# First layer of a two-layer kernel: scan output summed by transposes, layer norm with positions on partitions, gate projections of 32 rows, and one ordered plan

## The chip, the cores and the metric

The kernel runs on one core of one Trainium2 chip. The metric is the device time in microseconds (us) of one execution, lower is better; several executions are timed and their median is compared. The core has a matrix engine (PE, with its weight loads shown apart as PEld), a vector engine (DVE), an activation engine (ACT), a general engine (POOL) and a queue engine that issues transfers (SP). Each works through its own list of instructions in order, and they wait for one another by semaphores. PE writes to PSUM, which has eight banks of 2 KB per partition here; POOL reads and writes SBUF alone.

## The reference

Two layers one after the other, on x of 8 x 192 x 64 x 64, all in fp32. The change is in the first; the second (layer norm over 192 channels and two state-space scans, forward and flipped) stays as it is. The first layer, per image:

```python
x = conv1x1(x, W_in)                          # 192 -> 384 channels
x = depthwise_conv3x3(x, W_dw) + b_dw
x_proxy = conv1x1(x, W_xd)                    # 16 channels
ws, Ls, Us, Ds = (conv1x1(x_proxy, w) for w in (W_w, W_l, W_u, W_d))
xs = [x, x.T, flip(x), flip(x.T)]             # 4 directions
Gl, Gm, Gr = ws[:nd], ws[nd:2*nd], ws[2*nd:]
s = abs(Gl) + abs(Gm) + abs(Gr) + 1e-7        # each gate is divided by s
# scan over 8 columns (j) of each of the 8 chunks of a row:
#   h = l * x + gl * h_up + gm * h + gr * h_down
out = gate_scan(xs, Ls, Gl, Gm, Gr, 8)
out = out * Us + xs * Ds
y = einsum('bdchw,d->bchw', out, w_m)         # sum over the 4 directions
y = layernorm2d(y, ln_w, ln_b)                # over the 384 channels
y = grn(y, gamma, beta)                       # global norm over positions per channel
return conv1x1(y, W_out)                      # 384 -> 192
```

## The kernel before, in words

The 384 channels lie on partitions as 3 tiles of 128 (c = 0, 1, 2). An image goes through three stages.

**Units** (class `Image`). There are 24 units, one for each c and each band r of 8 rows (512 positions). `begin` is two accumulating matmuls into a PSUM bank (tags gl, gm, q, yp in turn), three ACT passes (the middle tap with the bias, and the taps at the two sides) and two POOL additions; the other six taps of the 3 x 3 convolution are six DVE operations in `unit`. `proxy` projects a finished band to 16 channels, held four times, at partitions 0, 32, 64 and 96, as tile xp.

**Scan** (class `Step`). For each c, each j (0 to 7) and each direction d (0 to 3) there is one step on tiles of 128 x 512: 96 steps per image, 12 of them with j = 0, where the state begins and most parts do nothing. The parts of a step with j > 0 are:

- `gates`: four matmuls of 16 rows (`gate`), pl for the input's factor and g[0..2] for the three neighbours, each with its weights at another 32-row group. `up`: two more, pd and pu.
- `decay` (ACT copies pl to lam), `entry` (POOL: lam times x), `magnitude` (ACT: absolute values; that of g[2] in place), `norm` (DVE: two additions), `log`, `exp` (ACT), `newton` (DVE: two operations) for 1/s.
- `neighbour` 0, 1, 2 (DVE: gate times shifted state), `pair` (POOL: q0 + q1), `total` (PE: q2 + q0 by the identity), `mix` (DVE: times 1/s), `state` (POOL).
- `direct` (ACT copies pd), `bypass` (POOL: times x; for d = 3 it also adds the dx of d = 2, `JOINED`), `output` (DVE: pu times the state, giving hu).
- `add`: PE adds hu and dx into the bank yp by the identity, over the four directions of one j; the dx of d = 2 is left out since it is in that of d = 3. `store`: ACT copies yp to y after d = 3.

PSUM tags: gl, gm, q, yp have one bank each; gr and c have two. pl, pd and pu all take the tag "c". The state of a step is read by the step four later (same direction, next j).

The order on each engine is the program order (`manual_schedule`); across engines Tile puts in the waits, also for a PSUM slot that is still to be read. In `scan` the order is written out by hand: in one turn of the loop stand `s3`, `s2`, `s1`, `s0` and `ahead`, five steps one apart, and each part stands once.

**Norm and projection** (class `Norm`, `project_out`) of an image run while the units of the next one do: per j, three matmuls with a matrix of 1/384 give the mean on all partitions, DVE subtracts, ACT squares, three more matmuls give the variance, ACT and DVE make the inverse root, POOL scales, and ACT squares with a sum over positions for the global norm. `PARTS` and the loop at the end say how many units and projections stand between one another. After the last image the norm and the projection stand alone. The result goes to `mid` in DRAM, which the second layer reads.

Of the kernel before, what the change touches and what calls it, by code (L numbers as in the profile page):

```python
# [8 lines left out]
F32 = mybir.dt.float32  # L9
# [24 lines left out]
JOINED = 2  # L34
# [3 lines left out]
PARTS = [0] * 8 + [1, 1, 1, 2, 1, 1, 1, 1, 1, 1, 1, 1, 1, 1, 1, 1]  # L38
# [4 lines left out]
ROWS = {GL: (0, 0), GM: (1, 0), GR: (2, 0), GLAM: (3, 0), GU: (0, 1), GD: (1, 1)}  # L43

# [78 lines left out]
def kernel(ctx: ExitStack, tc: tile.TileContext, x, w_in, dw, vecs, w_xd, w_gate, w_m, w_out, mid):  # L123
# [9 lines left out]
    big = ctx.enter_context(tc.tile_pool(name="l0_big", bufs=6))  # L133
# [32 lines left out]
    w_gate_sb = const.tile([P, 2, ND, CI], F32, name="w_gate_sb")  # L166
    for kind, (group, at) in ROWS.items():
        nc.sync.dma_start(w_gate_sb[32 * group : 32 * group + RANK, at], w_gate[:, kind])
# [10 lines left out]


# [9 lines left out]
    class Image:  # L190
# [6 lines left out]
        def __init__(self, b):  # L197
            self.b = b
            self.x = x[b].rearrange("(k p) h w -> p k (h w)", p=KM)
            self.xc, self.xins, self.banks = [], {}, {}  # L200
            self.xp = p1.tile([P, CHUNK, CHUNK, HW], F32, tag="xp", name=f"xp_{b}")
            self.u = 0
            for u in range(4):
                self.load(u)
            for u in range(2):
                self.begin(u)
# [7 lines left out]
        def begin(self, u):  # L214
            c, r = divmod(u, CHUNK)
            if r == 0:
                self.xc.append(big.tile([P, HW, HW], F32, tag="big", name=f"xc_{self.b}_{c}"))
# [5 lines left out]
            self.load(u + 4)  # L223
# [26 lines left out]
        def proxy(self, r):  # L250
            pp = bank("c", f"pp_{self.b}_{r}")
            for c in range(NC):
                nc.tensor.matmul(
                    pp,
                    w_xd_sb[:, c, :],
                    self.xc[c][:, 8 * r : 8 * r + 8, :].rearrange("p h w -> p (h w)"),
                    start=(c == 0),
                    stop=(c == NC - 1),
                )
            nc.scalar.copy(  # L260
                self.xp[:, :, :, 8 * r : 8 * r + 8].rearrange("p j n h -> p h n j"),
                pp.rearrange("p (h n j) -> p h n j", n=CHUNK, j=CHUNK),
            )

        def unit(self):

            u, self.u = self.u, self.u + 1
            if u + 2 < UNITS:
                self.begin(u + 2)
            c = u // CHUNK  # L270
            for t in (0, 1, 2, 6, 7, 8):
                acc, part = self.shifted(u, t)
                nc.vector.scalar_tensor_tensor(
                    acc, part(self.banks[u]), dw_sb[:, c, t : t + 1], acc, ALU.mult, ALU.add
                )
            if u >= UNITS - CHUNK + 2:
                self.proxy(u % CHUNK - 2)
# [17 lines left out]
    class Step:  # L295
# [4 lines left out]
        def __init__(self, tag, xc, xp, wg, d, j):  # L300
            self.tag, self.xc, self.xp, self.wg, self.d, self.j = tag, xc, xp, wg, d, j
# [7 lines left out]
        def gate(self, kind, tag):  # L309
# [3 lines left out]
            r = slice(32 * group, 32 * group + RANK)  # L313
            nc.tensor.matmul(dst, self.wg[r, at, self.d, :], flat(self.xp[r, self.j]), start=True, stop=True)  # L314
# [37 lines left out]
        def norm(self):  # L352
            if self.j:
                for i in range(2):
                    nc.vector.tensor_add(self.g[2], self.g[2], flat(self.ab[i]))  # L355
# [11 lines left out]
        def newton(self):  # L367

            if self.j:
                s, rc = self.g[2], flat(self.rc)  # L370
                nc.vector.scalar_tensor_tensor(s, s, 1e-7, rc, ALU.add, ALU.mult)
                nc.vector.scalar_tensor_tensor(rc, s, 2.0, rc, ALU.subtract, ALU.mult)
# [16 lines left out]
        def bypass(self):  # L389
            nc.gpsimd.tensor_mul(self.dx, self.dx, direction(self.xc, self.d, self.j))  # L390
            if self.d == JOINED + 1:
                nc.gpsimd.tensor_add(self.dx, self.dx, self.before.dx)
# [5 lines left out]
        def add(self, i):  # L398


            if self.d == 0 and i == 0:
                self.yp = bank("yp", f"yp_{self.tag}")
            elif i == 0:
                self.yp = self.before.yp
            if i == 0 or self.d != JOINED:
                nc.tensor.matmul(
                    self.yp,
                    ident,
                    flat((self.hu, self.dx)[i]),
                    start=(self.d == 0 and i == 0),  # L410
                    stop=(self.d == ND - 1 and i == 1),
# [6 lines left out]
    class Nothing:  # L418


        def __getattr__(self, part):
            return lambda *args: None

    def scan(b, xc, xp):


        ys, steps = [], [Nothing()] * 4
        for c in range(NC):
            wg = w_gate_sb[:, :, :, c * P : (c + 1) * P]
            ys.append(big.tile([P, CHUNK, CHUNK * HW], F32, tag="big", name=f"y_{b}_{c}"))  # L430
            for j in range(CHUNK):
                steps += [Step(f"{b}_{c}_{j}_{d}", xc[c], xp, wg, d, j) for d in range(ND)]
                for step in steps[-ND:]:
                    step.y = ys[c][:, j, :]
        for before, step in zip(steps[4:], steps[5:]):
            step.before = before
        steps += [Nothing()] * 4
        for s3, s2, s1, s0, ahead in zip(steps, steps[1:], steps[2:], steps[3:], steps[4:]):
            s2.state()
            s0.neighbour(2)  # L440
            s0.neighbour(0)
            s0.entry()
            s1.newton()
            s1.total()
            s0.neighbour(1)
            s0.pair()
            s0.magnitude(2)
            s2.direct()
            ahead.gates()
            s0.norm()  # L450
            s0.log()
            ahead.decay()
            s2.bypass()
            s3.add(0)
            s2.output()
            s3.add(1)
            ahead.magnitude(0)
            s1.up()
            s0.exp()
            s1.mix()  # L460
            ahead.magnitude(1)
            s3.store()
        return ys

    class Norm:


        def __init__(self, b, ys):
            self.b, self.ys = b, ys
            self.ss = p1.tile([P, NC, CHUNK], F32, tag="ss", name=f"ss_{b}")  # L470
            self.pm, self.squares, self.var, self.rstd = {}, {}, {}, {}

        def mean(self, j):
            self.pm[j] = bank("gr", f"pm_{self.b}_{j}")
            for c in range(NC):
                nc.tensor.matmul(self.pm[j], mean_w, self.ys[c][:, j, :], start=(c == 0), stop=(c == NC - 1))

        def center(self, j):
            for c in range(NC):
                y = self.ys[c][:, j, :]  # L480
                nc.vector.tensor_sub(y, y, self.pm[j])
                sq = self.squares[j, c] = p2.tile(
                    [P, T], F32, tag=("ab0", "ab1", "dx")[c], name=f"sq_{self.b}_{j}_{c}"
                )
                nc.scalar.activation(sq, y, AF.Square)

        def variance(self, j):
            self.var[j] = bank("c", f"pv_{self.b}_{j}")
            for c in range(NC):
                nc.tensor.matmul(self.var[j], mean_w, self.squares[j, c], start=(c == 0), stop=(c == NC - 1))  # L490

        def root(self, j):

            r = self.rstd[j] = p2.tile([P, T], F32, tag="rc", bufs=3, name=f"rstd_{self.b}_{j}")
            v = self.var[j]
            nc.scalar.activation(r, v, AF.Ln, bias=eps5)
            nc.scalar.activation(r, r, AF.Exp, scale=-0.5)
            nc.vector.scalar_tensor_tensor(v, v, 1e-5, r, ALU.add, ALU.mult)
            nc.vector.tensor_mul(v, v, r)
            nc.vector.scalar_tensor_tensor(r, v, 3.0, r, ALU.subtract, ALU.mult)  # L500

        def response(self, j):

            for c in range(NC):
                y = self.ys[c][:, j, :]
                sq = p2.tile([P, T], F32, tag="hu", name=f"sq2_{self.b}_{j}_{c}")
                nc.scalar.activation(
                    sq,
                    y,
# [6 lines left out]
        def scale(self, j):  # L516
            for c in range(NC):
                y = self.ys[c][:, j, :]
                nc.gpsimd.tensor_mul(y, y, self.rstd[j])

        def parts(self):

            for j in range(CHUNK + 2):
                if j < CHUNK:
                    self.mean(j)
                if 0 <= j - 1 < CHUNK:
                    self.root(j - 1)
                    self.scale(j - 1)
                if j > 1:
                    self.response(j - 2)  # L530
                if j < CHUNK:
                    self.center(j)
                yield
                if j < CHUNK:
                    self.variance(j)

    def project_out(b, ys, ss):

        gr = p1.tile([P, NC + 1], F32, tag="gr", name=f"gr_{b}")
        gx, rg = gr[:, :NC], gr[:, NC:]  # L540
        nc.vector.tensor_reduce(gx, ss, AX.X, ALU.add)
        nc.scalar.activation(gx, gx, AF.Sqrt)
        nc.scalar.preload_act_table_set(ACT_SET)
        yield
        pg = bank("c", f"pg_{b}", (P, 1))
        for c in range(NC):
# [564 lines left out]
```

## Time and profile before

| | |
|---|---|
| median of 3 runs | 16562.87 us (16551.99 to 16567.64) |
| the profiled execution | 16565.53 us, its span 16563.7 us |
| mean granted clock of PE | 0.923 of full |
| busy, whole span | PE 14978.0, DVE 14708.4, ACT 11718.0, POOL 14908.0 us |
| last transfer to `mid` issued (first layer ends) | 5978.3 us |
| stores of y of image 2, first and last | 1652.8 and 2175.8 us |
| first store of y of image 3 | 2383.5 us |

A line of a group view reads: line, engine, operation, out<-in by the program's names, shapes, count, then busy us and mean ns of one, then the idle time of the engine just before them and what ended most of it. A line of the timeline reads: start us, duration us, engine, line, operation, operands, count, and in brackets the idle time before it and what ended that. A matmul with fp32 operands is two records on PE, a transpose one. Ends of PE's records are modelled, so starts are the better measure there.

### The profile page before, as it was taken

What the parts mean: (1) busy time and instruction counts of PE and PEld (TensorE: products, weight loads), DVE (VectorE), ACT (ScalarE), POOL (GpSimd) and SP (SyncE); (2) the same over time, 40 slices, a digit from 0 to 9 for tenths busy, and PEclk for the clock granted to TensorE, in tenths of its full rate; (3) what the DMA queues carried; (4) which work ended last, traced back from release to release, by engine and by line L of the source; (5) the groups of instructions that cost most, each with busy time, mean ns of one, the idle gap of its engine ahead of it and who ended that gap; (6) DMA issues with size and microseconds to landing.
All of it is one profiled execution on the core that took longest, in us unless ns stands there. A gap on an engine that the chain in (4) does not pass through costs nothing.

```text
span 16563.7 us, 198688 instructions
## 1 busy us (share of the span) xinstructions
PE 14978.0 (90%) x66768; PEld 8677.0 (52%) x66768; DVE 14708.4 (89%) x13970; ACT 11718.0 (71%) x25475; POOL 14908.0 (90%) x9292
## 2 busy tenths in 40 slices
PE   9999999999999978888888888888888888888888
PEld 2333333333333346666666666666666666666666
DVE  8887888788888859999999999999999999999999
ACT  5666666666656657777777777777777777777777
POOL 7887979787787859999999999999999999999999
PEclk8999999999999989999999999999999999989999
DMA  1001010100000012222323232222222222222232
GB/s 30 21 11 31 1 31 1 31 11 21 27 4 27 1 61 109 108 109 111 115 110 116 108 113 109 108 109 108 109 108 109 108 109 108 109 108 112 108 115 98
DMA packets 732369, 1260.72 MB, mean 76 GB/s; under 512 B 346905, under 2 KB 415345, under 8 KB 731345
## 3 DMA queue, kind: packets, MB, share of 16 engines
q1 hardware_dynamic: 730944, 1247.72, 20.6%
q8 instruction: 526, 8.62, 0.2%
q14 instruction: 499, 4.08, 0.1%
q10 hardware_dynamic: 400, 0.29, 0.0%
HBM read 1189.11 MB, written 58.72 MB: 75 GB/s over the span
## 4 chain that ended last, share of the span: by engine, by line
POOL 23%; PE 10%; ACT 10%; DVE 9%; issue 6%; DMA 4%; SPq 0%; POOLq 0%; DVEq 0%; ACTq 0%
POOL hs L963 16%; DVE da L979 5%; POOL hs L986 5%; PE pc L785 4%; ACT da L969 3%; DMA b_sb<-bc 3%; DVE hs L979 2%; PE yp L991 2%; PE pz L795 2%; PE pj L864 2%; DVE hs L986 2%; POOL dtx L877 1%; DMA c_sb<-bc 1%; ACT xc L806 1%; ACT z L807 1%
## 5 line engine op out<-in xcount | busy, mean ns | idle before, releaser
L963 POOL TENSOR_TENSOR hs<-dtx,b_sb 128x1022 f32<-128x1022 f32 x3072 | 7183.6, 2361 | 139.1 <-DMA b_sb<-bc 118.4
L979 DVE TENSOR_TENSOR_SCAN da<-da,hs 128x1024 f32<-128x1024 f32 x2048 | 4686.7, 2288 | 408.3 <-POOL hs L963 309.4
L969 ACT ACTIVATE da<-dt,a 128x512 f32<-128x512 f32 x6144 | 4247.6, 691 | 61.8
L991 PE MATMUL yp<-ident,hs 128*128 128x128 f32 x24576 | 3377.6, 290 | 89.7 <-POOL hs L986 68.6
L991 PEld LDWEIGHTS yp<-ident,hs 128*128 128x128 f32 x24576 | 2993.9, 150 | 625.9 <-issue 359.4
L979 DVE TENSOR_TENSOR_SCAN hs<-da,hs 128x1024 f32<-128x1024 f32 x1024 | 2314.1, 2280 | 316.4 <-ACT da L969 228.1
L986 DVE TENSOR_TENSOR hs<-da,c_sb 128x1024 f32<-128x1024 f32 x2048 | 2499.9, 1221 | 62.2 <-DVE da L979 0.5
L986 POOL TENSOR_TENSOR hs<-hs,c_sb 128x1024 f32<-128x1024 f32 x1024 | 2418.5, 2362 | 3.9 <-ACT state L982 3.9
L785 PE MATMUL pc<-xT,conv 128*128 128x512 f32 x4608 | 2165.2, 603 | 69.3 <-ACT xT L758 66.7
L314 PE MATMUL g<-xp,w_gate_sb 16*128 16x512 f32 x8640 | 1817.2, 658 | 60.4 <-ACT dx L387 51.6
L340 DVE TENSOR_TENSOR q<-g,h 128x512 f32<-128x512 f32 x2016 | 1353.1, 685 | 117.8 <-PE g L314 71.2
L350 PE MATMUL q<-q,ident 128*128 128x512 f32 x2688 | 1337.7, 620 | 0.0
L785 PEld LDWEIGHTS pc<-xT,conv 128*128 128x128 f32 x4608 | 813.5, 191 | 981.4 <-issue 858.1
L360 ACT ACTIVATE rc<-g,eps 128x512 f32<-128x512 f32 x672 | 462.0, 688 | 1114.2 <-DVE g L355 1114.2
L390 POOL TENSOR_TENSOR dx<-dx,xc 128x512 f32<-128x512 f32 x768 | 1079.9, 1406 | 156.9 <-ACT dx L387 133.4
L982 ACT COPY state<-da 128x2 f32<-128x2 f32 x2048 | 322.8, 158 | 1267.2 <-DVE hs L986 1256.6
L314 PEld LDWEIGHTS g<-xp,w_gate_sb 16*128 16x128 f32 x8640 | 494.0, 188 | 1308.0 <-DVE q L340 392.2
L864 PE MATMUL pj<-ident,lg 128*128 128x128 f32 x1536 | 555.5, 362 | 561.3 <-ACT lg L858 561.3
L344 POOL TENSOR_TENSOR q<-q,q 128x512 f32<-128x512 f32 x672 | 853.6, 1270 | 199.5 <-DVE q L340 193.7
L334 POOL TENSOR_TENSOR lam<-lam,xc 128x512 f32<-128x512 f32 x672 | 942.7, 1403 | 32.9 <-ACT lam L331 32.9
L355 DVE TENSOR_TENSOR g<-g,ab 128x512 f32<-128x512 f32 x1344 | 933.5, 695 | 22.8
L795 PE MATMUL pz<-in_w,xT 128*128 128x384 f32 (+1 forms) x2048 | 855.6, 520 | 82.4 <-ACT xc L787 79.1
(148 smaller groups left out, 26031.3 us busy)
## 6 DMA issues: line engine op xcount, KB each, us to landing
b_sb<-bc SPq DMA_DIRECT2D x1024, 512.0 KB, 10.2
c_sb<-bc SPq DMA_DIRECT2D x1024, 512.0 KB, 10.1
xin<-in_x_dram SPq DMA_DIRECT2D x192, 384.0 KB, 3.6
mid<-ot SPq DMA_DIRECT2D x128, 192.0 KB, 2.1
xt<-mid SPq DMA_DIRECT2D x64, 384.0 KB, 10.0
out_dram<-y SPq DMA_DIRECT2D x64, 384.0 KB, 9.9
xt<-mid SPq DMA_DIRECT2D x64, 128.0 KB, 9.1
bc<-dbl SPq DMA_DIRECT2D x128, 64.0 KB, 1.7
```

What stands on the lines that cost most here:

```text
L314: nc.tensor.matmul(dst, self.wg[r, at, self.d, :], flat(self.xp[r, self.j]), start=True, stop=True)
L334: nc.gpsimd.tensor_mul(self.lam if self.j else self.hc, self.lam, direction(self.xc, self.d, self.j))
L340: nc.vector.tensor_mul(self.q[i], rows(self.g[i]), self.h[:, :, i : i + HW])
L350: nc.tensor.matmul(self.sum, ident, flat(term), start=(i == 0), stop=(i == 1))
L390: nc.gpsimd.tensor_mul(self.dx, self.dx, direction(self.xc, self.d, self.j))
L785: nc.tensor.matmul(self.pc[c], w[:, n, :], x[:, k, at : at + T], start=(n == 0), stop=(n == 5))
L795: nc.tensor.matmul(pi, self.tokens.xT[r, i, 3 + s * P : 3 + (s + 1) * P], self.m.in_w[r, i, :], start=(i == 0), stop=(i == 1),)
L963: nc.gpsimd.tensor_mul(self.hs[:, :, 1:], dtx, self.p.b_sb[self.g][:, :, 1:])
L969: nc.scalar.activation(self.da[:, n, :], self.p.dt[self.c], AF.Exp, scale=self.p.m.a[:, self.c, at : at + 1])
L979: nc.vector.tensor_tensor_scan(h, da, hs, 0.0, ALU.mult, ALU.add)
L986: engine.tensor_mul(self.hs, self.h, self.p.c_sb[self.g])
L991: nc.tensor.matmul(self.p.yp[self.c][:, s, :], self.hs[:, n, s * P : (s + 1) * P], ident, is_transpose=True, start=False, stop=(self.g == ...
```

## The change

- The order of the whole first layer comes from tables of slots. Every part of every unit, step and norm gets a number (its base plus the table's entry) and all are issued in the order of these numbers. Step k of an image stands at slot 28 + k, and images are 128 slots apart. `newton` and `norm` are split into their two operations.
- `add` turns hu and dx in four pieces of 128 x 128 by transposing matmuls that accumulate in yp, so y has positions on partitions and channels along the free dimension. The joined dx is gone.
- Layer norm: `bn_stats` and `bn_aggr` over 384 channels per block of 128 positions, an inverse root of small tiles per two j, scaling on POOL, and `back`, which transposes to channels on partitions (12 transposes per j) and copies and squares from PSUM on ACT.
- `gate` uses 32 rows; the gate weights are set to zero first, so rows 16 to 31 add nothing.
- xc and y are one array each and no longer six buffers.

```diff
+STEPS = NC * CHUNK * ND
+PERIOD = UNITS + 8 + STEPS
+UNIT_PLAN = {
+    "load": [(-4.6, ())],
+    "begin": [(-2.1, ())],
+    "taps": [(0.4, (0,)), (-0.5, (1,))],
+}
+PROXY_PLAN = [20.7, 21.0, 20.5, 20.8, 22.5, 23.0, 23.9, 23.7]
+NORM_PLAN = {
+    "stats": [(-1.7, (0,)), (-0.75, (1,)), (0.4, (2,)), (0.65, (3,)), (2.0, (4,)), (3.35, (5,)), (4.0, (6,)), (4.75, (7,))],
+    "root": [(-0.55, (0,)), (2.15, (1,)), (4.25, (2,)), (6.15, (3,))],
+    "scale": [(0.6, (0,)), ..., (7.35, (7,))],
+    "back": [(2.8, (0,)), (3.25, (1,)), ..., (7.5, (6,)), (8.45, (7,))],
+    "leave": [(9.7, (0,)), (10.35, (1,)), (11.0, (2,))],
+    "project": [(12.3, (0, 0)), (13.75, (0, 1)), ..., (26.3, (6, 0)), (27.95, (6, 1)), (29.0, (7, 0)), (31.25, (7, 1))],
+}
+STEP_PLAN = {
+    "neighbour 0": 0.04, "entry": 0.04, "neighbour 1": 0.12, "newton 0": 1.12, "total": 1.14,
+    "newton 1": 1.16, "pair": 0.16, "magnitude 2": 0.18, "add 0": 3.19, "norm 0": 0.2,
+    "gates": -0.76, "add 1": 3.3, "decay": -0.6, "magnitude 0": -0.6, "norm 1": 0.41, "log": 0.43,
+    "mix": 1.46, "magnitude 1": -0.5, "neighbour 2": -0.49, "up": 1.53, "output": 2.69, "exp": 0.77,
+    "bypass": 2.84, "direct": 1.86, "store": 3.96, "state": 1.98,
+}
...
-    big = ctx.enter_context(tc.tile_pool(name="l0_big", bufs=6))
...
     w_gate_sb = const.tile([P, 2, ND, CI], F32, name="w_gate_sb")
+    nc.gpsimd.memset(w_gate_sb, 0.0)
     for kind, (group, at) in ROWS.items():
         nc.sync.dma_start(w_gate_sb[32 * group : 32 * group + RANK, at], w_gate[:, kind])
...
+    xc_all = const.tile([P, NC, HW, HW], F32, name="xc_all")
+    y_all = const.tile([P, CHUNK, NC * T], F32, name="y_all")
+    yT = y_all.rearrange("p j (s c) -> p j s c", c=CI)
+    y_of = [y_all.rearrange("p j (c t) -> p c j t", t=T)[:, c] for c in range(NC)]
...
-            r = slice(32 * group, 32 * group + RANK)
-            nc.tensor.matmul(dst, self.wg[r, at, self.d, :], flat(self.xp[r, self.j]), start=True, stop=True)
+            r = slice(32 * group, 32 * group + 32)
+            nc.tensor.matmul(dst, self.wg[r, at, self.d, :], flat(self.image.xp[r, self.j]), start=True, stop=True)
...
         def bypass(self):
             nc.gpsimd.tensor_mul(self.dx, self.dx, direction(self.xc, self.d, self.j))
-            if self.d == JOINED + 1:
-                nc.gpsimd.tensor_add(self.dx, self.dx, self.before.dx)
...
-            if i == 0 or self.d != JOINED:
+            term = flat((self.hu, self.dx)[i])
+            for s in range(BLOCKS):
                 nc.tensor.matmul(
-                    self.yp,
+                    self.yp[:, s, :],
+                    term[:, s * P : (s + 1) * P],
                     ident,
-                    flat((self.hu, self.dx)[i]),
-                    start=(self.d == 0 and i == 0),
-                    stop=(self.d == ND - 1 and i == 1),
+                    is_transpose=True,
+                    start=(self.d == 0 and i == 0 and s == 0),
+                    stop=(self.d == ND - 1 and i == 1 and s == BLOCKS - 1),
                 )
...
+        def stats(self, j):
+            ...
+            for s in range(BLOCKS):
+                st = p2.tile([P, 6], F32, tag="st", name=f"st_{self.b}_{j}_{s}")
+                nc.vector.bn_stats(st, yT[:, j, s, :])
+                nc.vector.bn_aggr(self.mv[pair][:, j % 2 * BLOCKS + s, :], st)
+
+        def scale(self, j):
+            for s in range(BLOCKS):
+                y, at = yT[:, j, s, :], j % 2 * BLOCKS + s
+                nc.gpsimd.tensor_scalar(
+                    y, y, self.rstd[j // 2][:, at : at + 1], self.mv[j // 2][:, at, 0:1], ALU.mult, ALU.add
+                )
+
+        def back(self, j):
+            ...
+            for c in range(NC):
+                pt = bank(("gr", "gr", "c")[c], f"pt_{self.b}_{j}_{c}")
+                for s in range(BLOCKS):
+                    nc.tensor.transpose(pt[:, s * P : (s + 1) * P], yT[:, j, s, c * P : (c + 1) * P], ident)
+                banks.append(pt)
+            for c in range(NC):
+                nc.scalar.copy(y_of[c][:, j, :], banks[c])
+                sq = p2.tile([P, T], F32, tag="hu", name=f"sq_{self.b}_{j}_{c}")
+                nc.scalar.activation(sq, banks[c], AF.Square, ..., accum_out=self.ss[:, c, j : j + 1])
...
+            for k, step in enumerate(steps):
+                for part, slot in STEP_PLAN.items():
+                    part, *args = part.split()
+                    at(base + UNITS + 4 + k + slot, getattr(step, part), *map(int, args))
...
     with tc.manual_schedule():
+        for _, _, part, args in sorted(plan, key=lambda entry: entry[:2]):
+            part(*args)
```

## The prediction, made before the change was run

> **What bounds the kernel now.** I read first the busy times by stretch (core 0; busy us and count for PE, PEld, DVE, ACT, POOL, then granted clock, DMA share, GB/s): an even stretch of image 2's scan, then its handover to image 3 in four pieces.
>
> ```profile
> 1653.00:1791.00 138.00, 138.00 (x471) 45.01 (x469) 135.36 (x217) 92.50 (x175) 132.24 (x102) 1.00 0.00 1
> 2176.00:2252.00 76.00, 60.34 (x136) 24.67 (x134) 60.68 (x90) 60.40 (x115) 48.73 (x41) 1.00 0.18 52
> 2252.00:2305.00 53.00, 50.64 (x115) 21.73 (x116) 48.74 (x77) 35.17 (x49) 27.41 (x24) 0.84 0.36 104
> 2305.00:2352.00 47.00, 45.90 (x108) 18.97 (x107) 28.10 (x39) 24.70 (x28) 9.89 (x9) 1.00 0.15 44
> 2352.00:2384.00 32.00, 31.28 (x85) 10.07 (x84) 18.85 (x30) 16.72 (x32) 24.61 (x19) 0.79 0.13 35
> ```
>
> PE never stops in the scan, but DVE and POOL are within 4% of it. The stores of y (L416) lie 22.96 us apart for four steps: 5.74 us a step. From the last store of one image to the first of the next it is 208 us. The second layer, from 5981 us on, is not touched.
>
> Next the timeline of one step on PE (start, duration, line; two records are one fp32 matmul of the program):
>
> ```profile
> 1700.94 1.14 PE L314 MATMUL g<-xp,w_gate_sb 16*128 16x512 f32 x8
> 1702.01 1.12 PE L406 MATMUL yp<-hu,ident 128*128 128x512 f32 x2
> 1702.97 1.02 PE L406 MATMUL yp<-dx,ident 128*128 128x512 f32 x2
> 1703.92 1.13 PE L314 MATMUL g<-xp,w_gate_sb 16*128 16x512 f32 x4
> 1704.98 1.98 PE L350 MATMUL q<-q,ident 128*128 128x512 f32 x4
> 1706.89 0.71 PE L314 MATMUL g<-xp,w_gate_sb 16*128 16x512 f32 x4
> ```
>
> From start to start: gates 1.07 (four matmuls in four row groups, side by side), hu 0.96, dx 0.95, `up` 1.06, `total` 1.91: 5.95. A step without its own dx (one in four) is shorter by 0.85 to 0.95, so the mean is 5.72. The order on PE itself is the period.
>
> DVE's nine operations of a step start 0.60 to 0.62 apart, but 0.724 where the second reads what the first wrote (L355 after L355, L372 after L371): 5.69 a step.
>
> Third, what a slot of the PSUM tag "c" (two slots: pl, pd, pu) does where engines wait, at the start of j = 1:
>
> ```profile
> 2008.28 0.59 ACT L387 COPY dx<-g 128x512 f32<-128x512 f32 x1 [0.97 <-PE g L314]
> 2008.92 1.14 PE L314 MATMUL g<-xp,w_gate_sb 16*128 16x512 f32 x8 [0.72 <-ACT dx L387]
> 2010.08 0.58 ACT L331 COPY lam<-g 128x512 f32<-128x512 f32 x1 [0.37 <-PE g L314]
> 2010.21 0.69 DVE L340 TENSOR_TENSOR q<-g,h 128x512 f32<-128x512 f32 x1 [0.63 <-PE g L314]
> ```
>
> The gates stand 0.72 us until `direct` has read pd, and start 0.05 us after its end; the first reader on ACT starts 1.16 us after them, on DVE 1.29.
>
> Last, the price of an accumulating fp32 transpose, in the second layer, which has the form that `add` gets:
>
> ```profile
> 8003.16 1.09 PE L991 MATMUL yp<-ident,hs 128*128 128x128 f32 x8
> 8004.09 0.59 PE L785 MATMUL pc<-xT,conv 128*128 128x512 f32 x1
> ```
>
> Eight take 0.93 us to the next matmul's start, 0.12 each (0.109 between two).
>
> **The change, part by part. Adds.** hu and dx cost 1.75 matmuls of 0.95 = 1.67 us of PE a step; now 8 transposes of 0.11 to 0.125, taken as 0.50 for each four, 1.0 in all. PE's sum falls to 1.07 + 1.06 + 1.91 + 1.0 = 5.04. The row stands at 0.109 us, at a granted clock of 1.00. Against this change speaks the Trainium skill ("TensorE: Matmul & The Clock Gate", Part 4): about 275 ns for a transpose within a kernel (bf16), and transposes do not count as activity that keeps the clock up. By its figure the eight would be 2.2 us and PE's sum 6.24, an estimate. The sum here goes by the row.
>
> **The join.** The addition of two dx on POOL (L392, 192 x 1.27 us) goes; POOL falls from about 5.5 to 5.2 us a step. POOL is not last, so I count 0.
>
> **32 rows.** The four gates stay in four row groups, so duration 0. They matter for the clock. From the trace's records I weighted each matmul's streaming time by rows/128 in each 3.41 us interval between clock changes: at full clock, an interval below 0.36 was followed by half clock and one above was not, in 99.4% of intervals; transposes count in full in this fit. The lowest interval of the new step (worked out below: one with the idle 1.2 us, `up` and some matmuls around) has 0.42 to 0.44 with 32 rows, some 0.27 with 16.
>
> **The order of a step.** This decides. By phase in a slot the new plan gives PE: total(t-1), add 0(t-3), gates(t+1), add 1(t-3), up(t-1); DVE: neighbour 0(t), newton 0(t-1), neighbour 1(t), newton 1(t-1), norm 0(t), norm 1(t), mix(t-1), neighbour 2(t+1), output(t-2). `up` (1.53) of a step now comes before `output` (2.69) of the step before it; until now `output` came first. With two "c" slots, up(t-1) needs the slot of pu(t-2), which output(t-2) reads. So PE waits in `up` for DVE, and behind it stand total(t), add 0(t-2) and gates(t+2). But output(t-2) stands on DVE behind neighbour 2(t+1), which needs gates(t+1). From neighbour 2's start n to the next gates: 0.61 to output, 0.685 its duration, 0.055 to PE, up 1.06, total 1.91, add 0.50 = 4.82. From gates to n: at least 1.29; and from the gates before that: ACT 1.16 to decay, then 0.465, 0.488, 0.585, 0.49 start to start and exp's own 0.64 with 0.06 to newton 0, then 0.608 + 0.598 + 0.608 + 0.724 + 0.608 + 0.598 on DVE = 7.64. With period P, P = 4.82 + max(1.29, 7.64 - P), so P = 6.23; by the first path alone 6.11. I take 6.2, range 6.0 to 6.4 (transposes at 0.43, a latency hidden; or a store in the way). PE idles 1.2 us in front of `up`. 84 of 96 steps of an image have these operations: 672 x (6.2 - 5.74) = **+309 us** (+175 to +444).
>
> **Steps with j = 0** have no DVE chain. PE there falls by 0.9 us at full clock; 96 steps make -86, to twice that at half clock, or nothing where POOL (two products, 2.8 us) and latency set the time. I take **-60** (-170 to 0).
>
> **Norm and handover.** Of PE go 6 matmuls per j (mean, variance; 48 x 0.95 = 46 us an image); 12 transposes per j come (96 x 0.11 = 11 us). DVE: 3 subtractions and 3 Newton operations of 0.69 go; 4 statistics come (192 wide 0.335 us; 384 wide between that and 0.67, taken as 0.53) and 4 aggregations of 0.18: 2.7 us per j with their overlap, 22 an image against 33. ACT: 6 x 0.69 and two of 0.69 become 3 copies (0.48) and 3 squares with their accumulator read (0.9): 4.15 us per j. POOL: 3 x 1.27 becomes 4 scalings 128x384, not in this trace; bounds 0.4 (a memset of that size) and 0.95 (1.27 x 384/512), taken as 0.65, plus seven small ones of 0.2 per pair. Now the chain per j takes 8.3 us and holds the units back: 78 us from the last output to the last response. In the new plan ACT is last: 5.65 slots x 1.8 + 33 + 2 = 45 us after 25 us of DVE (five statistics and 2.5 units of 4.1), 70 to 72 us, with two more units done. What follows is PE's: up to the first gates 13.4 begins x 1.9 + 8 proxies and 13 projections of 2.85 = 85 us, plus 11 idle where only units run: 97, against 100 now. The gain is 9 us, and 4 more since three projections move into the first steps where PE waits: 13 x 7 handovers = **-91** (0 to -350, the latter if the handover closes up to PE's sum of 125 us). After image 7 norm and projections stand alone, 128 us; norm's 74 become 45 to 50: **-25** (-10 to -40).
>
> **Start.** The memset of the gate weights, 128x3072, costs 3 us of POOL by the 415 ns of 128x384. Six weight loads on SP wait for it, and behind them the first image's loads: **+3**. Memory: the single xc and y arrays are read and written in the same order as the six buffers; 0.
>
> Sum: 309 - 60 - 91 - 25 + 3 = +136. The profiled execution took 16565.5 us (span 16563.7) and the median is 16562.9, so the sum is 2.7 us less against the median: about 16700.
>
> **The rivals.** (1) Faster: the slot of pu does not bind and DVE becomes the bound. The place is `up`; it turns where output(t-2) ends within 1.55 us after the gates start (gates and add 1), 1.1 us earlier than my walk has it. Newton is now parted by neighbour 1, so DVE's step is 5.69 - 0.12 = 5.57; 672 x -0.17 = -114, total -287: 16276. For it: PE's sum of 5.04. Against it: the 0.72 us wait above shows the tag binds. (2) The scan slows as forecast, but the handover closes up: 43 x 7 = -301 in place of -91 makes 16490. Against it: the third and fourth lines of the table are already 95 to 98% PE. (3) The clock falls in the scan, where 0.42 is close to 0.36: one interval at half costs PE 1.7 us; every third step makes 224 x 1.7 = +380: 17080. Against it: in the rule it needs intervals a sixth lower.
>
> **How the numbers follow.** Forecast 0.58, rival 1 0.17, rival 2 0.12, rival 3 0.07, and 0.06 for a scan loss and handover gain that cancel within 0.2% (33 us, about what a measurement of this kernel can tell from no change). Faster: 0.17 + 0.12 = 0.29; same 0.06; slower 0.65. The forecast alone, with its bounds combined, has 16530 to 16870. The range reaches to rival 1 and leaves rival 3 out: 16280 to 16890.
>
> **What would show it.** Right: stores 24.8 us apart (four steps); PE idle about 1.2 us ahead of `up`, ended by DVE hu; clock 1.00 in the scan; transposes of hu and dx 0.11 apart; last store to first store some 195 us. Wrong: stores 22.4 apart and PE waiting elsewhere, DVE without gaps (rival 1); 165 us between images (rival 2); clock under 0.9 in even stretches (rival 3).

## The result, and the profile after

The changed kernel takes **16681.03 us** (median of 4 runs, 16675.44 to 16717.93) against 16565.25 us for the kernel before in the same comparison (4 runs, 16551.99 to 16574.58). The ratio is 1.0075, 95% interval 1.0058 to 1.0093: slower by 0.75%. The profiled execution took 16678.27 us, its span 16676.5 us.

The starts of the stores of y (L478 now, L416 before), 24 to an image, divide the span into stretches that can be compared one by one. The prediction's terms go by steps, so they are laid on the stretches here: 4 x 0.46 = 1.84 us for each of the 168 groups of four steps with j > 0 (16 of them lie in the row of j = 0), and 60 / 96 = 0.625 us off each of the 96 steps with j = 0 (64 lie in that row, 28 in the handovers, 4 in the start).

| stretch of the span, us | before | after | difference | predicted |
|---|---|---|---|---|
| start to the first store | 171.4 | 176.4 | +5.0 | 0 (+3 - 2.5) |
| scans, even four-step groups, 144 of them, mean | 22.98 | 25.33 | 144 x 2.35 = +338 | 144 x 1.84 = +265 |
| scans, last group of an image, 8 of them | 14.3 | 16.83 | +20 | +15 |
| scans, two groups around the steps with j = 0, 16 of them | 49.26 | 42.87 | 16 x -6.39 = -102 | -11 (+29 - 40) |
| handovers, last store to next first store, sum of 7 | 1469.2 | 1348.8 | -120 | -108 (-91 - 17.5) |
| last store to last transfer to `mid` | 125.8 | 96.8 | -29 | -25 |
| second layer | 10585.4 | 10586.0 | +0.6 | 0 |

The sum is +113 in the spans; the prediction said +136. The median of the even groups is 24.89 us (predicted: 24.8), and a quarter of them, 36 of 144, are about 1.7 us longer than that.

The busy times by stretch (window, its length, then busy us and count for PE, PEld, DVE, ACT, POOL, granted clock, DMA share, GB/s) of the changed kernel: an even stretch of image 2's scan, the 27 us after it, its steps with j = 0, and its handover to image 3.

```profile
1669.00:1743.00 74.00, 72.51 (x288) 29.48 (x287) 66.23 (x108) 44.40 (x87) 62.50 (x48) 1.00 0.00 1
1743.00:1770.00 27.00, 26.49 (x98) 10.77 (x98) 22.96 (x37) 15.49 (x31) 21.43 (x17) 0.94 0.00 1
1819.60:1863.40 43.80, 42.37 (x153) 18.29 (x153) 25.30 (x41) 20.34 (x39) 32.37 (x25) 0.88 0.00 1
2237.00:2429.00 192.00, 162.35 (x446) 72.02 (x446) 141.12 (x231) 119.92 (x207) 103.59 (x124) 0.88 0.21 62
```

By the first line PE is still 98% busy, DVE and POOL no longer are (89% and 84%; before 98% and 96%). Someone who reads only this line would say that PE is the bound and that its work has become longer. The timeline of one step on PE says otherwise (start, duration, engine, line):

```profile
1701.67 1.14 PE L377 MATMUL g<-xp,w_gate_sb 32*128 32x512 f32 x8
1702.75 0.66 PE L467 MATMUL yp<-ident,dx 128*128 128x128 f32 x4
1703.53 2.16 PE L377 MATMUL g<-xp,w_gate_sb 32*128 32x512 f32 x4
1705.62 1.98 PE L413 MATMUL q<-q,ident 128*128 128x512 f32 x4
1707.44 0.60 PE L467 MATMUL yp<-ident,hu 128*128 128x128 f32 x4
1707.97 1.14 PE L377 MATMUL g<-xp,w_gate_sb 32*128 32x512 f32 x8
```

The four gates (x8 records) still cost 1.08 us from start to start, four transposes cost 0.53 (hu, to the gates), `total` 1.82. But `up` (x4), two matmuls, costs 2.09 where it cost 1.06 before. The weight loads of the same step show why:

```profile
1702.74 0.42 PEld L467 LDWEIGHTS yp<-ident,dx 128*128 128x128 f32 x4 [0.76 <-POOL q L407]
1703.53 0.29 PEld L377 LDWEIGHTS g<-xp,w_gate_sb 32*128 32x128 f32 x2 [0.36 <-ACT lam L394]
1704.56 0.29 PEld L377 LDWEIGHTS g<-xp,w_gate_sb 32*128 32x128 f32 x2 [0.74 <-issue]
```

and on ACT and DVE, what they wait for:

```profile
1702.89 0.59 ACT L394 COPY lam<-g 128x512 f32<-128x512 f32 x1 [2.52 <-PE g L377]
```

```profile
1699.44 0.70 DVE L434 SCALAR_TENSOR_TENSOR g<-g,rc 128x512 f32<-128x512 f32 x1 [0.68 <-ACT rc L427]
1700.04 0.68 DVE L403 TENSOR_TENSOR q<-g,h 128x512 f32<-128x512 f32 x1
1700.64 0.68 DVE L434 SCALAR_TENSOR_TENSOR rc<-g,rc 128x512 f32<-128x512 f32 x1
1701.24 1.43 DVE L417 TENSOR_TENSOR g<-g,ab 128x512 f32<-128x512 f32 x2
1702.57 0.68 DVE L438 TENSOR_TENSOR rc<-q,rc 128x512 f32<-128x512 f32 x1
1703.17 0.68 DVE L403 TENSOR_TENSOR q<-g,h 128x512 f32<-128x512 f32 x1
1703.77 0.68 DVE L456 TENSOR_TENSOR hu<-g,h 128x512 f32<-128x512 f32 x1
1704.36 0.68 DVE L403 TENSOR_TENSOR q<-g,h 128x512 f32<-128x512 f32 x1
1705.59 0.70 DVE L434 SCALAR_TENSOR_TENSOR g<-g,rc 128x512 f32<-128x512 f32 x1 [0.54 <-ACT rc L427]
```

The two matmuls of `up` used to run side by side. Now pd starts at 1703.53, when `decay` has given back its "c" slot (ACT's copy ends at 1703.48), and pu at 1704.56, when `output` of the step before has given back the other (DVE's product, L456, ends at 1704.45). In between PE counts as busy with pd alone. So the wait of the forecast is there, as 0.2 us ahead of pd and 1.03 us within `up`, and the group view hides it: of the idle time before this line, 96.9 us in all, it puts 6.5 us down to DVE hu.

```profile
L377 PE MATMUL g<-xp,w_gate_sb 32*128 32x512 f32 x8640 | 2455.9, 650 | 96.9 <-DVE hu L456 6.5
```

In the kernel e5 below, where the wait is gone, the same matmuls are busy for less, with the same mean of one; what is missing is the time in which one ran without its neighbour:

```profile
L377 PE MATMUL g<-xp,w_gate_sb 32*128 32x512 f32 x8640 | 1997.1, 658 | 7.5 <-ACT ot L590 1.8
```

What holds `output` back is DVE's own list. `mix` (L438) and `neighbour 2` (L403) run right ahead of it, and DVE has no gap from the first `newton` operation (L434 at 1699.44), which waits 0.68 us for ACT's `exp` (rc L427), to `output` (L456 at 1703.77). So the loop runs from the gates over ACT to `exp`, over DVE to `output`, and over `up`, `total` and `add` back to the gates: one round in two steps.

The second line of the stretches has the surprise, a clock of 0.94 in an even stretch. One `total` in it takes 3.60 us and not 1.98:

```profile
1749.11 1.98 PE L413 MATMUL q<-q,ident 128*128 128x512 f32 x4
...
1755.41 3.60 PE L413 MATMUL q<-q,ident 128*128 128x512 f32 x4
```

The even groups hold 39 such drops, often 88.7 us apart, each one interval of the clock long (3.41 us). They make the 36 longer groups: 0.44 us on the mean group, 144 x 0.44 = 63 us.

### The profile page after: what moved, and what is told of

The parts are those of the page before. It is cut to its first block, busy times and chain, and to the rows that moved or that the text cites. A ratio compares the mean times of both kernels' runs of the same rounds, so it can differ in the third digit from the quotient of the medians.

```text
span 16676.5 us, 206100 instructions
## 1 busy us (share of the span) xinstructions
PE 14970.9 (90%) x70224; PEld 9108.0 (55%) x70224; DVE 14603.9 (88%) x14098; ACT 11578.2 (69%) x25411; POOL 14667.0 (88%) x9389
## 4 chain that ended last, share of the span: by engine, by line
POOL 23%; PE 11%; ACT 9%; DVE 9%; issue 7%; DMA 5%; SPq 0%; POOLq 0%; DVEq 0%; ACTq 0%
POOL hs L980 16%; POOL hs L1003 6%; DVE da L996 5%; PE pc L802 4%; DMA b_sb<-bc 4%; ACT da L986 3%; PE pz L812 2%; PE yp L1008 2%; DVE hs L996 2%; DVE hs L1003 1%; PE pj L881 1%; POOL dtx L894 1%; DMA c_sb<-bc 1%; ACT xc L823 1%; ACT z L824 1%
## 5 line engine op out<-in xcount | busy, mean ns | idle before, releaser
L377 PE MATMUL g<-xp,w_gate_sb 32*128 32x512 f32 x8640 | 2455.9, 650 | 96.9 <-DVE hu L456 6.5
L394 ACT COPY lam<-g 128x512 f32<-128x512 f32 x768 | 451.4, 588 | 1856.9 <-PE g L377 1856.9
L403 DVE TENSOR_TENSOR q<-g,h 128x512 f32<-128x512 f32 x2016 | 1373.5, 682 | 239.6 <-PE g L377 208.0
L413 PE MATMUL q<-q,ident 128*128 128x512 f32 x2688 | 1418.8, 653 | 0.0
L377 PEld LDWEIGHTS g<-xp,w_gate_sb 32*128 32x128 f32 x8640 | 693.3, 186 | 902.4 <-issue 589.2
L452 POOL TENSOR_TENSOR dx<-dx,xc_all 128x512 f32<-128x512 f32 x768 | 1078.4, 1404 | 22.6 <-ACT dx L449 20.8
L397 POOL TENSOR_TENSOR lam<-lam,xc_all 128x512 f32<-128x512 f32 x672 | 941.5, 1401 | 109.3 <-ACT lam L394 106.7
L413 PEld LDWEIGHTS q<-q,ident 128*128 128x128 f32 x2688 | 474.8, 196 | 860.0 <-issue 716.4
```

The lines of the kernel that those rows point to most:

```text
L377: nc.tensor.matmul(dst, self.wg[r, at, self.d, :], flat(self.image.xp[r, self.j]), start=True, stop=True)
L397: nc.gpsimd.tensor_mul(self.lam if self.j else self.hc, self.lam, direction(self.xc, self.d, self.j))
L403: nc.vector.tensor_mul(self.q[i], rows(self.g[i]), self.h[:, :, i : i + HW])
L413: nc.tensor.matmul(self.sum, ident, flat(term), start=(i == 0), stop=(i == 1))
```

## The experiments

The theory (A): PE reaches `up` before `output` of the step before has read its slot; the place of `output` decides, and the rest of the change is a gain. Its rivals: gate matmuls of 32 rows make `up` last 2.1 us by themselves (R1); and in later runs what their texts name. All times are medians; before took 16569.59 us beside e1 to e4 and 16570.85 us beside e5 to e8 (7 runs each). "Even" is the median four-step group, "j = 0" the mean of the two groups around such steps, "handover" the sum of seven, from the profile of each.

| kernel | us | ratio to before (95%) | even | j = 0 | handover |
|---|---|---|---|---|---|
| e1_output_first | 16185.09 | 0.9769 (0.9755 to 0.9784) | 22.38 | 38.74 | 1341.6 |
| e2_output_exp | 16140.29 | 0.9742 (0.9727 to 0.9756) | 22.07 | 39.60 | 1343.1 |
| e3_rows16 | 18210.84 | 1.0986 (1.0952 to 1.1019) | 33.85 | 56.45 | 1385.1 |
| e4_old_step_order | 16218.99 | 0.9790 (0.9775 to 0.9804) | 22.75 | 39.20 | 1355.0 |
| e5_output_in_norm | 16049.24 | 0.9686 (0.9671 to 0.9701) | 21.56 | 39.05 | 1342.3 |
| e6_best_rows16 | 16248.56 | 0.9805 (0.9789 to 0.9820) | 21.56 | 49.78 | 1340.2 |
| e7_best_projections_first | 16039.12 | 0.9681 (0.9664 to 0.9699) | 21.56 | 38.77 | 1329.9 |
| e8_up_key | 16685.90 | 1.0074 (1.0058 to 1.0090) | 24.89 | 42.56 | 1350.7 |

**e1: output ahead of the next up.** On DVE `output` now stands ahead of `mix` and `neighbour 2`; no other engine's list changes.

```diff
-    "output": 2.69,
+    "output": 2.45,
```

> The changed kernel with one number changed: output of a step at 2.45 in place of 2.69, so that on DVE it stands before mix and neighbour 2, and ahead of the up that reuses its PSUM slot. Theory A (PE waits in up for the slot of pu, which output reads, and output waits behind neighbour 2 for the gates): the loop gates, neighbour 2, output, up, total, add is cut; the next longest loop runs from the gates over ACT (decay to exp, 3.83 us), newton 0, neighbour 1, newton 1 (to 5.80) back to the gates, 5.86 us a step, so 23.4 us per four steps in place of 24.9; the granted clock in even stretches 1.00; about 16380 us (16320 to 16450). Rival R1 (pd and pu with 32 rows no longer run side by side, up costs 2.1 us in any order, and PE's own list is the period): 24.9 us as before and 16680 us. Rival R2 (the chain over exp to neighbour 2 and not the slot sets the period): no change, 16680 us.

One number of the table is worth 496 us against the changed kernel, and turns 0.75% slower into 2.3% faster. `up` of 32 rows lasts as long as that of 16 rows did, which ends R1:

```profile
1582.53 1.13 PE L377 MATMUL g<-xp,w_gate_sb 32*128 32x512 f32 x4 [0.22 <-DVE hu L456]
1583.59 1.98 PE L413 MATMUL q<-q,ident 128*128 128x512 f32 x4
```

`up` costs 1.06 us again, and 0.22 us of the wait is left. The theory's size was off: it expected about 16380 from a loop of 5.86 us a step through exp and newton back to the gates. The step is 22.38 / 4 = 5.60 us: DVE's own sum, 5.52 by its starts (1.33 for the two of norm, 0.60 for each of seven others), and 0.3 us a group in which DVE waits. I had made all four gates wait for newton; in the table only the tile of g[2] is held until newton has read the sum of the magnitudes. That this is the reason was read from the table and not tested.

**e2: exp earlier as well.**

```diff
-    "output": 2.69,
+    "output": 2.45,
-    "exp": 0.77,
+    "exp": 0.45,
```

> As the run with output at 2.45, and exp at 0.45 in place of 0.77, so that ACT does it right after log and before magnitude 1. Theory A: the loop over exp is shorter by 0.49 us (5.37), DVE's nine operations are the longest with 5.57 us, 22.3 us per four steps; about 16180 us (16120 to 16280). Rival R1 (up is 2.1 us with 32 rows in any order): 24.9 us and 16680 us. Rival R2 (the chain over exp alone is the bound): here faster than the run with output alone by all of the 0.49 us a step, while that run shows nothing.

Even groups of 22.07 us, 4 x 5.52 (22.3 expected), and 45 us less than e1: the rest of DVE's waiting has gone. The earlier `exp` was not run without the earlier `output`.

**e3: the changed kernel with gates of 16 rows.** It asks what the 32 rows are worth in the changed order, with its wait.

```diff
-            r = slice(32 * group, 32 * group + 32)
+            r = slice(32 * group, 32 * group + RANK)
```

> The changed kernel with gate projections of 16 rows as before the change, all else kept. Theory A with the clock rule read from the trace of before (an interval of 3.41 us in which streaming time weighted by rows/128 stays under 0.36 is followed by half clock): the lowest interval of a step falls from about 0.38 to 0.25, so the clock falls in the scan about every second step, 1.7 us each: 17250 us (16900 to 17500), granted clock in the scan clearly under 0.95. Rival R1 (32 rows cost time since pd and pu no longer run side by side): up falls from 2.1 to 1.06 us, 1 us a step less, about 16200 us.

The sign is that of the clock rule, the size is 2.7 times what was expected (+570): 1530 us more than the changed kernel. The stretch from 2076 to 2230 us is even scan:

```profile
2076.00:2230.00 154.00, 152.24 (x453) 61.67 (x452) 107.47 (x170) 70.15 (x136) 100.09 (x76) 0.71 0.00 0
```

Within the scans half clock lasted 3836 of 5943 us. The rule held. Take the streaming time of a record as 0.109 us for 128 columns (the prediction's row), twice that at half clock, and weight it by rows/128: then 214 of the 511 full-clock intervals of the even groups lie below 0.36, and each of these was followed by half clock, as were 6 of the 297 others. What was wrong was how long a drop lasts. The expectation had 336 drops of one interval; there were 262 in the scans, of 4.2 intervals on average and up to 22. At half clock the same matmuls stream for twice as long, and a bound at 0.785, that is twice 0.39, parts the 898 half-clock intervals of the even groups: in 887 of them half clock stayed below it and full clock followed above it. In the changed kernel each of the 39 drops was over after one interval.

**e4: parts of a step in the order of the kernel before**, with the transposes, the new norm, the 32 rows and the new plan of units, norm and handover kept. All entries of the step's table are replaced; those that matter:

```diff
-    "gates": -0.76,
+    "gates": -0.595,
-    "add 0": 3.19,
-    "add 1": 3.3,
+    "add 0": 3.615,
+    "add 1": 3.685,
-    "up": 1.53,
-    "output": 2.69,
+    "up": 1.755,
+    "output": 2.650,
...
```

> The changed kernel with the parts of a step in the order of the kernel before (output ahead of up, newton and norm each in one piece, bypass and adds where they stood); transposes, norm, handover and 32 rows are those of the change. Theory A: no wait for the slot of pu; PE's list is 5.0 us, DVE's nine operations with two dependent pairs 5.69 us set the step: 22.8 us per four steps (22.96 in the kernel before), and with the handovers and the steps of j = 0 of the change about 16240 us (16180 to 16330). Rival R1 (up costs 2.1 us with 32 rows in any order): PE's list 6.1 us, 24.5 us per four steps, about 16650 us.

16219 us, within 0.13% of what was expected. It separates the change into two: all but the order of the parts gains 2.1%, the order of the parts alone gives back 2.9% (1.0075 over 0.9790). It also shows where the gain of the cheaper adds went. PE's own list for a step fell from 5.72 to about 5.1 us (gates 1.08, hu 0.53 and `total` 1.82 as above, `up` 1.06 as in e1, dx 0.59 as in e5), but the group only from 22.98 to 22.75 us, because DVE's nine operations still take 5.69 us, with two pairs in which the second reads what the first wrote:

```profile
1604.57 0.69 DVE L434 SCALAR_TENSOR_TENSOR g<-g,rc 128x512 f32<-128x512 f32 x1
1605.29 0.69 DVE L434 SCALAR_TENSOR_TENSOR rc<-g,rc 128x512 f32<-128x512 f32 x1
1605.90 0.68 DVE L403 TENSOR_TENSOR q<-g,h 128x512 f32<-128x512 f32 x1
1606.50 1.42 DVE L417 TENSOR_TENSOR g<-g,ab 128x512 f32<-128x512 f32 x2
1607.83 0.68 DVE L456 TENSOR_TENSOR hu<-g,h 128x512 f32<-128x512 f32 x1
```

From newton 0 to newton 1 it is 0.72 us, over the two of norm 1.33 us; elsewhere 0.60.

**e5: output between the two of norm.** If DVE is the bound, parting the last dependent pair must be worth what the pair costs.

```diff
-    "output": 2.69,
+    "output": 2.3,
-    "exp": 0.77,
+    "exp": 0.45,
```

> Two entries of the step's table: output of a step from 2.69 to 2.3, exp from 0.77 to 0.45. As in e2_output_exp no output stands behind the next up, and on DVE output now lies between norm 0 and norm 1, so that of the pairs in which an operation reads what the one before it wrote none is left in a step. Theory (DVE's nine operations are the bound once the wait in front of up is gone, and a dependent neighbour costs 0.724 us in place of 0.608): 0.116 us a step less than e2's 22.07 us per four, so 21.6 us between stores; 672 x -0.116 = -78 us, so about 16060 us (16030 to 16110). Rival (another loop or POOL's 5.2 us a step is what binds e2): 22.07 us between stores, and 16140 us.

Even groups of 21.56 us (21.6 expected) and 16049 us (16060). The stretch from 1517 to 1625 us has DVE busy for all of it, and DVE's starts now are evenly 0.60 apart (9 x 0.60 = 5.4 us a step; 21.56 / 4 = 5.39):

```profile
1517.00:1625.00 108.00, 107.88 (x482) 48.72 (x480) 108.00 (x182) 77.41 (x147) 104.43 (x81) 1.00 0.00 1
1646.40:1686.90 40.50, 39.47 (x154) 17.45 (x152) 25.02 (x42) 20.79 (x40) 32.07 (x25) 0.87 0.00 1
```

```profile
1539.79 0.70 DVE L417 TENSOR_TENSOR g<-g,ab 128x512 f32<-128x512 f32 x1
1540.39 0.69 DVE L456 TENSOR_TENSOR hu<-g,h 128x512 f32<-128x512 f32 x1
1540.99 0.70 DVE L417 TENSOR_TENSOR g<-g,ab 128x512 f32<-128x512 f32 x1
```

Once the wait is gone DVE binds the even scan, and POOL, busy for 104.43 of 108 us, may be next; that wasn't tested. PE's 107.88 us say little, since its busy time holds waits within matmuls.

**e6: e5 with 16 rows.** The same line as in e3, in an order without the wait.

> e5_output_in_norm with gate projections of 16 rows instead of 32. Clock rule from the trace of before (an interval of 3.41 us whose streaming time weighted by rows/128 is below 0.36 is followed by half clock): without the wait in front of up PE's activity is spread evenly, the lowest interval has about 0.44 by rows of 16, so the clock stays at 1.00 in the even scan and the time is that of e5 within 0.2%, about 16060 us. Rival (gates of 16 rows let the clock fall in this order whatever the wait, as e3_rows16 did): stores over 24 us apart, over 16500 us.

Half right. In the even scan the clock stays at 0.98 and the median group at 21.56 us, where the same edit had cost the changed kernel 9 us a group; so there it was the wait that made 32 rows matter. But the total is 199 us above e5, and the rows with j = 0 have most of it, 16 x (49.78 - 39.05) = 172 us. Nearly all the rest is in the even groups, which hold 20 drops of the clock: their lowest intervals have some 0.40 (counted as in e3) and not the expected 0.44, and their mean is 0.20 us above e5's, 29 us in all. The first line is the even stretch, the second the j = 0 steps, to be set beside e5's second line above:

```profile
1576.00:1685.00 109.00, 108.91 (x481) 49.38 (x480) 107.79 (x181) 76.95 (x146) 104.06 (x81) 0.98 0.00 1
1706.40:1754.30 47.90, 46.67 (x154) 19.34 (x152) 25.51 (x42) 20.84 (x39) 32.21 (x25) 0.71 0.00 1
```

The clock there is 0.71 against 0.87. PE is busy for 97% of both stretches with the same 154 matmul records, and length times clock is nearly the same, 34.0 and 35.2 us, so the time follows the clock.

**e7: three projections ahead of the next image's first gates.**

```diff
-        (26.3, (6, 0)), (27.95, (6, 1)), (29.0, (7, 0)), (31.25, (7, 1)),
+        (26.3, (6, 0)), (26.6, (6, 1)), (26.9, (7, 0)), (27.1, (7, 1)),
```

It is made on e5.

> e5_output_in_norm with the last three projections of an image at slots 26.6, 26.9 and 27.1 instead of 27.95, 29.0 and 31.25, that is, ahead of the next image's first gates and not within its first steps. Theory of the prediction (three projections that move into the first steps, where PE waits, are worth 4 us a handover): 4 x 7 = +28 us against e5, up to +60 if all their 3 x 2.85 = 8.6 us of PE come to stand in the way. Rival (PE has other waits there and the place makes no difference): within 10 us of e5.

10 us less than e5, not 28 more, and by the profile the handovers became 12.4 us shorter in all. The ranges of runs overlap (16026.8 to 16046.9 and 16043.0 to 16057.0), so I read it as no loss, perhaps a small gain. That the projections are worth 4 us a handover inside the first steps is refuted, as far as e5's order can tell. e7 is also the shortest of the kernels run, 3.2% under the kernel before.

**e8: another place for up across engines.** Every engine's own list stays as it was; only the issue order between engines moves.

```diff
-    "up": 1.53,
+    "up": 1.75,
```

> The changed kernel with the table's entry of up at 1.75 in place of 1.53. The order of the instructions on each engine stays what it was; what moves is the place of up in the program's order across engines: add 1 of four steps back is at 3.3, so up and what lies between change only against the other engines' lists. Theory (the loss is the order on PE and DVE: PE reaches up before output has read the slot): nothing changes, 24.9 us between stores, about 16680 us (16650 to 16710). Rival (the program's order across engines decides which slot's reader a wait is put on, so a later up finds a slot that is free): 22.4 to 23 us between stores, 16380 us or less.

16685.9 us and 24.89 us between stores: the same. With `up` at 1.75 the table has `output` of the step before (2.69 less one step, 1.69) ahead of it, as e1 has, and nothing is gained. So it isn't the order of these two entries that decides but `output`'s place in DVE's own list, which e1 changes and e8 doesn't.

## Why the prediction was right, by its own steps

**The order of a step** was the step that decided, and it held. The wait for pu's slot came where the walk put it, behind `output`, which stands behind `neighbour 2`, and by the longer of the walk's two branches, the one over `exp`: a round of two steps was to take 4.82 + 7.64 = 12.46 us, and 2 x 24.89 / 4 = 12.45. The shorter branch alone had 6.11 us a step. e1 moves `output` forward on DVE and the loss goes. The prediction also names the table's order of `up` and `output`; by e8 that order by itself makes no difference. In detail the walk was simpler than the machine: it held all of `up` back until `output` had ended, while pd starts on `decay`'s slot and only pu waits; so PE's clean idle time of 1.2 us does not appear as such, but as 0.2 us of idle time and an `up` of 2.09 us.

**Adds.** 0.50 us for four transposes was the estimate; the starts say 0.53 for hu, and 0.59 for dx in e5. The figure of the Trainium skill ("TensorE: Matmul & The Clock Gate", Part 4), about 275 ns each, would make 1.1 us for four, an estimate; here the row of the second layer was the right price. That transposes don't count for the clock isn't what these traces show either: in e4 none of the 936 intervals of the even groups was followed by half clock. Their weighted streaming time is at least 0.56 with transposes counted in full; counted at nothing, the lowest would have 0.31, and in e3 each of the 214 below 0.36 was followed by half clock.

**32 rows** were counted at nothing, "duration 0", and the clock was said to stay at 1.00 because the lowest interval has 0.42 to 0.44. This step failed, in opposite directions at two places. In the even scan the interval was the right one, but too highly put: it holds the end of the gates, the transposes of dx, the wait, `up` and the first part of `total`, and has some 0.37, counted as in e3. Of the 1009 full-clock intervals of the even groups 110 lie below 0.39; 38 of these were followed by half clock, and 1 of the 899 others. That pd and pu run one after the other isn't the reason, for they count the same side by side. The drops are the +63 us, a small share of rival 3: it needed intervals a sixth lower, they came about an eighth lower, and the even groups have 39 drops where it had 224 in the scans. On the other side the rows seem to bring a gain in the j = 0 steps that the sum didn't have.

**Steps with j = 0** were the term that was furthest off. Without the mean even group beside them, four such steps took 49.26 - 22.98 = 26.3 us before and 42.87 - 25.33 = 17.5 after: 8.7 us less where the sum had 2.5, and outside its bounds (-170 for 96 steps is 7.1 for four). The sum gave the gain to PE's shorter adds. e6 puts it elsewhere: with 16 rows such a pair takes 49.78 us, no less than the 49.26 before, with 32 rows 39.05. The clock of that stretch was 0.80 before, is 0.88 after (third line of the first fence), 0.87 in e5 and 0.71 in e6:

```profile
1790.60:1841.40 50.80, 47.94 (x118) 14.52 (x116) 26.16 (x41) 20.64 (x40) 35.23 (x27) 0.80 0.00 0
```

As far as these orders can be compared, the shorter adds alone let the clock down by as much as they save, and the gain comes only with the rows. No run has 32 rows with the old adds, so what the rows are worth by themselves isn't shown.

**Norm and handover** were set at -13 each, and -15.5 with the four j = 0 steps that lie in the stretch; -17.2 came. The 4 us from moved projections aren't there, by e7. How the 17.2 us split between the norm and the j = 0 steps isn't shown. In the handover shown PE's busy time fell from 188 us of 208 (the four lines of the prediction) to 162 of 192, so PE stands idle for longer, 30 us and not 20, and what it saved came through only in part. Which wait of the new handover ends last wasn't tested by an experiment. Rival 2, 165 us between images, is refuted (193 us).

**Norm after image 7** (-29 for -25) and the **start** (+5 for +3, less 2.5 for the j = 0 steps in it) were near. POOL's scaling, priced between 0.4 and 0.95 and taken as 0.65 us, took 0.665; the statistics over 384 channels, taken as 0.53 us, 0.533.

**Rival 1** described the kernel that e1 makes: DVE as the bound at 5.57 us a step, where e1 has 5.60. Its place was right; the changed kernel was on the other side of it because of one entry in a table. Its condition was stricter than need be: in e1 `output` ends 2.2 us after the gates start, not 1.55, PE still waits 0.22 us ahead of `up`, and DVE is the bound all the same.

That the sum came so near, +136 for +113, is partly luck, since errors cancelled: +63 for the clock, not counted, and +15 on the wait itself (338 + 20 - 63 = 295 for 265 + 15 = 280), against -91 in the row of j = 0, -12 in the handovers and -4 at the end.

## What to carry to other kernels

When an order changes, list for each PSUM tag its slots in order of use, with the engine that reads each last, and walk the loop through the slots: a wait that comes from one operation's place ate more here (2.9%) than everything else in the change had gained (2.1%). An engine that is 98% busy may still be waiting within its matmuls, so compare one step from start to start before and after, not the busy shares. And a saving of matrix work can lower the granted clock: weigh each interval's matmuls by their rows before counting the saved time.

## What the runs showed of the hardware that I had not expected

- Rows of zeros are worth time. The same matmuls with 16 rows, and with 32 of which 16 are zeros, take 18211 against 16681 us in the changed order, and 16249 against 16049 us without its wait; the granted clock of the even stretch is 0.71 with 16 rows and the wait, 0.98 with 16 rows alone. The Trainium skill ("TensorE: Matmul & The Clock Gate", Part 1) ties the half clock to a window of about 3.4 us in which PE is idle; here PE was busy for 152 of 154 us and the clock was 0.71 all the same, so a busy share doesn't tell it; the rows do, as far as these runs go.
- Two matmuls in different row groups shared their time when they started together: the pair of `up` took 1.06 us from start to start, and 2.09 us when the second was held back by 1.03, by when the first was about over (a lone one of this size, hu before the change, took 0.96).
- After a drop the clock came back by the same measure as it fell, as far as e3 shows: below 0.39 of weighted streaming at full clock, or below twice that at half clock, the next interval was at half clock. In the changed kernel intervals from 0.36 to 0.39 went either way. A loop that falls can stay down, for up to 22 intervals in e3, where the even scan of the changed kernel was back after one.
- On DVE an operation of 128 x 512 that reads what the one before it wrote starts 0.72 us after it, one that doesn't 0.60. Parting such a pair by an unrelated operation gained that difference in full: 4 x 0.12 = 0.48 us a group by the estimate, 22.07 to 21.56 measured.
